# Loading residuals earlier and reordering the last block of an attention-plus-recurrence kernel

## The chip, the core and the metric

The kernel runs on one core of one Trainium2 chip. The metric is device time in microseconds (us) for one execution of the whole program. A core has five instruction queues that matter here: PE (TensorE, matrix products), DVE (VectorE), ACT (ScalarE), POOL (GpSimd), and SP, which only issues DMA transfers. Each queue runs its instructions strictly in order; an instruction that waits for another engine holds up all that stand behind it on its own queue.

## The reference

The input `x` has shape (4, 128, 64, 64): four batches, 128 channels, 4096 tokens each. Two layers are computed.

```
# layer 0: attention over tokens with 64-channel keys, queries, values; residual
q, k, v = wq @ x, wk @ x, wv @ x
x = x + wo @ (softmax(k.T @ q, over the second index) applied to v)

# layer 1, on tokens t of 128 channels
t = t + causal_attention(layernorm(t))          # 4096 tokens, 128 channels
w = layernorm(t) @ W.T                          # W is 128 x 128
w = (w - mean) * rsqrt(var + eps) * gamma + beta   # mean, var over all 4*4096 tokens
y[-1] = 0;  y[n] = sigmoid(w[n] + y[n-1] @ V.T)   # a recurrence over 4096 tokens
t = t + y
```

The last part couples everything: the normalization of `w` needs the statistics of all tokens of all batches, and the recurrence runs over all tokens.

## The kernel before, in words

**Attention.** For each batch the kernel first computes layer 0 and then layer 1. Scores are products on PE, exponentials run on ACT, row sums on DVE, and the second product runs on PE again. Layer 0 keeps three arrays per batch in the pool `batch`, made in `cols0`: `kr` (the keys and rows), `swap` (the same with its halves exchanged) and `v`. `finish1` ends a block of 512 tokens of layer 1: `first` normalizes and stores, `second` turns the block to channels by way of memory (`chans`, then `xhT`), `third` makes the product `wx_ps` with W and its statistics (`stats`). The sum x + attention, which the end needs again as residual, is stored to memory: by channel in `x2c` for batches 0 and 1 (`BY_C = 2`) and half of batch 2, by token in `x2t` for the rest. The memory pool frames decide where a buffer lies; waits are put in by a layer that follows which instruction writes and reads each region.

**The recurrence is cut up.** Each batch's 4096 tokens are divided into 256 chunks (`NCH`) of 16 steps (`STEPS`), and all chunks of a batch advance at once, so that one step of one batch is a 128x256 product. A chunk does not know its starting state. It is warmed up over some steps taken from the chunk before it; the map contracts fast, and the result is compared at the end against a tolerance (`judge`), with a slow general path for inputs where this fails. The steps come in three stages:

- *Early steps*, before the last block of the last batch is done. The statistics without that block are used (`ahead` makes `most` = scale, shift, shift_half and `near`, the scale as a diagonal matrix). There are `AHEAD = 3` of them, i = 0, 1, 2. A step i > 0 is `early_input` (product with `near`), `early_product` (product with V) and `early_sigmoid` (ACT). `WHOLE` lists the four parts whose data are there: batches 0, 1, 2 and seven eighths of batch 3. `LAST` is the remaining 32 columns of batch 3, which come out of `final_block`. Step 2 writes its states into `warmed`, which lies in the memory `joint`.
- *Warm steps* s = -6 to -1 in `step(b, s)`: product with V (`y_ps`, L1372), `z = scale * wx + product` on DVE (L1379), sigmoid with bias `shift` on ACT (L1383). They use the exact statistics of all tokens: `affine(mv, xrp, "all", False)` makes `scale` and `shift` after the last block. At s = -1 the state goes into `start`, and POOL copies a piece of it (L1385) before step 0 may begin.
- *Output steps* s = 0 to 15, the same three instructions for the four batches, and beside them `residual(s - 1)` (three transposes on PE at L1404, an addition on DVE at L1408, an output DMA) for the parts by token and `add(s)` (two additions on POOL at L1393 and L1395, output DMAs) for the parts by channel. From s = 1 on the order on every engine is the program's own (`pin` keeps an instruction in program order): steps of batches 0 to 3, then the residual.

**Order.** Instructions marked with `pin` keep their order. Others are placed by a scheduler in the layer that records the program, so the order on each engine is known from the built program and not from the source alone. `final_block` is written out by hand, all pinned:

```
early_product(2, *WHOLE[1])
product(0)
early_sigmoid(2, *WHOLE[1])
```

`product(k)` makes half k of the last block's product, its statistics (`ends`, L998) and a copy into `xs` on ACT (L1001).

**Loads of the end.** When the attention is over, SP issues the last block's stores, a first quarter of the by-token residuals `xr`, then `xc` (batches 0 and 1 by channel, two transfers of 2048 KB at L1331), then `xh` (1024 KB), then the rest of `xr`.

Of the kernel before, what the change touches and what calls it, by code (L numbers as in the profile page):

```python
# [369 lines left out]
def fast_path(  # L370
# [44 lines left out]
    xs = xpool.tile([P, B, N], F32, name="xs")  # L415


    x2c = dram.tile([P, BY_C * N + N // 2], F32, name="x2c")
    x2t = dram.tile([(B - BY_C) * N - N // 2, P], F32, name="x2t")
    by_c = lambda b, g: b < BY_C or b == BY_C and g < NB // 2  # L420
# [74 lines left out]
    grid = lambda t: t.rearrange("p (g c) -> p g c", c=CPB)  # L495
    pin = tc.keep_in_program_order

    def affine(mv, pool, name, halved=True):
# [3 lines left out]
        scale, shift, shift_half = one("scale"), one("shift"), halved and one("shift_half")  # L502
        nc.vector.tensor_scalar(var, mv[:, 1:2], BN_EPS, None, ALU.add)
        nc.gpsimd.tensor_tensor(y, var, mhalf[:, :1], ALU.pow)
        nc.vector.tensor_scalar(half, var, -0.5, None, ALU.mult)
        nc.vector.tensor_scalar(nmean, mv[:, 0:1], -1.0, None, ALU.mult)
        nc.vector.scalar_tensor_tensor(z, in0=y, scalar=half, in1=y, op0=ALU.mult, op1=ALU.mult)
        nc.vector.scalar_tensor_tensor(y, in0=z, scalar=1.5, in1=y, op0=ALU.add, op1=ALU.mult)
        nc.vector.tensor_tensor(scale, y, gamma, ALU.mult)
        if halved:  # L510
            nc.vector.scalar_tensor_tensor(
                shift_half, in0=nmean, scalar=scale, in1=beta_half, op0=ALU.mult, op1=ALU.add
            )
        nc.vector.scalar_tensor_tensor(shift, in0=nmean, scalar=scale, in1=beta, op0=ALU.mult, op1=ALU.add)
        return scale, shift, shift_half

# [10 lines left out]
    with tc.tile_pool(name="batch", bufs=1) as batch, tc.tile_pool(name="rows", bufs=2) as rowp, tc.tile_pool(  # L527
# [9 lines left out]
        def misc(name):  # L537
            return ps_m.tile([P, BLK], F32, tag="m", name=name)
# [37 lines left out]
        def cols0(b, m):  # L576

            bt = bs[b]  # L580
            if m == 0:
                bt.kr = batch.tile([P, 2, N // 2], F32, tag="kr", name="kr")
                bt.swap = batch.tile([P, N // 2], F32, tag="swap", name="swap")
                bt.v = batch.tile([P, NT // 2, 2, M], F32, tag="v", name="v0")
            for h, w in enumerate((wkq, wqk)):
                if (b, m, h) == (0, 1, 1):
                    ps = ps_a.tile([P, 2, BLK], F32, tag="a", name="kr_ps")[:, 0]
                else:
                    ps = misc("kr_ps")
# [207 lines left out]
        def early_place(i, b, g0, g1):  # L797

            if not early:
                early.extend(halves.tile([P, 2, BLK], F32, tag="half", name="early") for _ in range(AHEAD - 1))  # L800
                early.extend(ps_s.tile([P, 2 * BLK], F32, tag="s", name="early_ps") for _ in range(2))
            cols = slice(g0 * CPB, g1 * CPB)
            bank, half = (b - 1, 1) if g0 and i == AHEAD - 1 else (b, i % 2)
            at = early[AHEAD - 1 + bank % 2][:, ds(bank // 2 * BLK + half * NCH, NCH)][:, cols]
            return cols, at, by_step[:, b, i - AHEAD - WARM + STEPS, g0:g1]

# [5 lines left out]
        def early_product(i, b, g0, g1):  # L812

            cols, at, _ = early_place(i, b, g0, g1)
            pin(nc.tensor.matmul(at, lhsT=vf, rhs=early_states(i - 1, b)[:, cols], start=False, stop=True))  # L815
# [62 lines left out]
        def finish1(b, g, turn):  # L878
            agg, den = bs[b].agg, bs[b].den
            mem = {}  # L880

            def first():
                denominators(1, b, g, mem["own"])
                joined(1, b, g, mem["op"] if turn else projected1(agg))
                by_tokens(b, g)
                mem["xh"] = wk.tile([P, TPB, P], F32, tag="xh2", name="xh2")
                mem["of"] = moments(b, g)

            def norm():
                normed(b, g, mem["xh"], *mem["of"])  # L890

            def second():
                mem["xhT"] = wk.tile([P, BLK], F32, tag="xhT2", name="xhT2")
                chans = dram2.tile([P, BLK], F32, tag="chans", name="chans")
                stored(mem["xh"], chans)
                nc.sync.dma_start(out=mem["xhT"], in_=chans)

            def kept():

                stored(xs[:, b, ts(g, BLK)].rearrange("p (j c) -> p j c", c=P), x2c[:, ds(b * N + g * BLK, BLK)])  # L900

            def third():

                wp = misc("wx_ps")
                nc.tensor.matmul(wp, lhsT=wf, rhs=mem["xhT"], start=True, stop=True)  # L905
                nc.vector.bn_stats(stats[:, b * NB + g], wp)
                if b == B - 1 and g == NB - 2:
                    ahead()
                    in_range(False)
                nc.scalar.copy(xs[:, b, ts(g, BLK)].rearrange("p (s c) -> p s c", s=STEPS), wp.rearrange("p (c s) -> p s c", s=STEPS))  # L910

            def sums():
                mem["own"] = folded(den, g < 2)
# [27 lines left out]
        def final_block(b, g, agg, den):  # L941
# [72 lines left out]
            early_input(2, *WHOLE[1])  # L1014
            turned(1)
            early_product(2, *WHOLE[1])
            product(0)
            early_sigmoid(2, *WHOLE[1])
            early_input(2, *WHOLE[2])
            product(1)  # L1020
            in_range(True)
            early_product(2, *WHOLE[2])
            early_input(2, *WHOLE[3])
            early_product(2, *WHOLE[3])
            early_input(1, *LAST)
            early_input(2, *LAST)
            early_sigmoid(0, *LAST)
            for i in range(1, AHEAD):
                early_sigmoid(2, *WHOLE[1 + i])
                early_product(i, *LAST)  # L1030
                early_sigmoid(i, *LAST)

# [279 lines left out]
    with tc.tile_pool(name="xr", bufs=1) as xrp, tc.tile_pool(name="y", bufs=2) as yp, tc.tile_pool(  # L1312
# [8 lines left out]
        xc = xrp.tile([P, BY_C, NCH, STEPS], F32, name="xc")  # L1321
        xh = xrp.tile([P, P, STEPS], F32, name="xh")
        xr = xrp.tile([P, UNITS, STEPS, P], F32, name="xr")

# [2 lines left out]
                pin(nc.sync.dma_start(out=xr[:, m, part], in_=by_chunk(x2t)[:, m, part]))  # L1327

        load_by_token(slice(0, STEPS // 4))
        for b in range(BY_C):  # L1330
            pin(nc.sync.dma_start(out=xc[:, b].rearrange("p k s -> p (k s)"), in_=x2c[:, ts(b, N)]))  # L1331
        pin(nc.sync.dma_start(out=xh.rearrange("p k s -> p (k s)"), in_=x2c[:, ds(BY_C * N, N // 2)]))
        load_by_token(slice(STEPS // 4, STEPS))

        mv = xrp.tile([P, nc.vector.BN_AGGR_DIM], F32, name="mv")
        nc.vector.bn_aggr(mv, ends)
        scale, shift, _ = affine(mv, xrp, "all", False)
        start = xrp.tile([P, B, Q + 1, NCH // Q], F32, name="start")
        nc.gpsimd.memset(start[:, :, 0, 1:2], 0.0)
        ended = lambda b: start[:, b, 1:].rearrange("p q (g w) -> p g q w", g=NB)  # L1340
# [58 lines left out]
        def residual(s):  # L1399
# [8 lines left out]
            pin(nc.vector.tensor_tensor(t, t, ps, ALU.add))  # L1408
            pin(nc.sync.dma_start(out=by_chunk(out_t)[:, :, s], in_=t))

        met = ps_m2.tile([P, BY_C, NCH], F32, name="met")
        gap = xrp.tile([P, B], F32, name="gap")
        tol = xrp.tile([P, B], F32, name="tol")
# [4 lines left out]
        for s in range(-WARM, STEPS):  # L1418
            for b in range(B):
                step(b, s)  # L1420
            if s >= 1:
                residual(s - 1)
            if TPB <= s < TPB + BY_C:
                b = s - TPB
                pin(nc.scalar.copy(by_row(met[:, b]), ended(BY_C + b)))
            if 0 <= s < STEPS - 1:
                add(s)

# [30 lines left out]
        count = xrp.tile([P, B + 2], F32, name="count")  # L1459
        nc.vector.tensor_copy(count[:, B:], good)  # L1460

        def judge():
            total = xrp.tile([P, 1], F32, name="total")
# [87 lines left out]
```

## Time and profile before

| what | value |
|---|---|
| time, median of 4 runs | 2007.0 us (2006.48 to 2007.11) |
| profiled execution, its own time | 2006.34 us |
| its span, first to last instruction | 2004.6 us |
| granted TensorE clock | 1.000 |
| PE, DVE, ACT, POOL busy | 100%, 73%, 49%, 7% of the span |
| last attention instruction on ACT (exponential) | starts at 1939.32 us |
| first warm sigmoid on ACT (L1383) | starts at 1955.04 us |
| first output sigmoid (s = 0, batch 0) | starts at 1966.07 us |
| flag of `judge` written (L1470) | starts at 2001.18 us |

The profile page is a single execution, with times from its own first instruction. A busy engine in it is one on which an instruction is in flight; products overlap, so PE counts as busy even when it gives no more than a part of its rate. A row of the timeline has start, duration, engine, line, operation, tiles written and read, shapes and count, and in brackets the idle time before it with what ended that.

### The profile page before, as it was taken

The page shows a single profiled execution, that of the slowest core. Times are in us where ns is not written, and L with a number is a line of the kernel's source. Part 1 is how long each engine was busy: PE and PEld are TensorE (multiplying, and loading weights), DVE is VectorE, ACT ScalarE, POOL GpSimd, SP SyncE. Part 2 cuts the span into 40 slices and gives each one's busy share as a digit, 9 for nine tenths or more (in the row PEclk, how much of TensorE's full clock was granted, in tenths as well). Part 3 has the DMA queues.
Part 4 walks back from the last instruction along what each step waited for, and adds up shares of the span by engine and source line. Part 5 has one row for each costly group of instructions (what it writes and reads, how often), then busy time and mean ns, then how long its engine had stood idle before and what let it go on. Part 6 is the DMA issues. An engine that isn't in the chain of part 4 may idle for free.

```text
span 2004.6 us, 31348 instructions
## 1 busy us (share of the span) xinstructions
PE 1998.6 (100%) x11864; PEld 873.4 (44%) x11864; DVE 1456.4 (73%) x2823; ACT 973.7 (49%) x1053; POOL 142.8 (7%) x253
## 2 busy tenths in 40 slices
PE   9999999999999999999999999999999999999999
PEld 3333354444333345444433334444443333544457
DVE  5799877555789987655588998664468998774569
ACT  5666633332666653333466664323356666333348
POOL 0000011000000001000000001000000000110016
PEclk9999999999999999999999999999999999999999
DMA  3111112310110111320111111222010111120018
GB/s 106 44 33 23 22 33 59 78 28 16 43 52 15 23 23 38 71 73 16 43 22 59 23 18 27 55 64 58 16 44 2 23 23 23 33 54 17 17 51 308
DMA packets 220027, 89.03 MB, mean 44 GB/s; under 512 B 142688, under 2 KB 204512, under 8 KB 219488
## 3 DMA queue, kind: packets, MB, share of 16 engines
q1 hardware_dynamic: 219584, 86.82, 17.4%
q8 instruction: 94, 1.54, 0.3%
q14 instruction: 61, 0.50, 0.1%
q10 hardware_dynamic: 288, 0.16, 0.0%
HBM read 45.84 MB, written 36.89 MB: 41 GB/s over the span
## 4 chain that ended last, share of the span: by engine, by line
PE 99%; DVE 0%; ACT 0%; issue 0%; POOL 0%; ACTq 0%; POOLq 0%
PE s_ps L1080 23%; PE acc L1140 22%; PE s_ps L1065 22%; PE acc L1129 22%; PE y_ps L1372 2%; PE o_ps L694 1%; PE r_ps L653 1%; PE wx_ps L905 1%; PE kr_ps L590 1%; PE v_ps L602 1%; PE o_ps L704 1%; PE yT_ps L1404 0%; PE warm_ps L544 0%; PE early_ps L810 0%; PE early_ps L815 0%; PE vT_ps L628 0%
## 5 line engine op out<-in xcount | busy, mean ns | idle before, releaser
L1109 DVE TENSOR_TENSOR dsum<-dsum,p 128x1024 f32<-128x1024 f32 x692 | 845.0, 1221 | 399.1 <-ACT p L1083 293.0
L1074 ACT ACTIVATE p<-s_ps,nshift 128x1024 f32<-128x1024 f32 x512 | 569.7, 1116 | 310.8 <-PE s_ps L1065 284.0
L1083 ACT ACTIVATE p<-s_ps 128x1024 f32<-128x1024 f32 (+2 forms) x288 | 274.3, 952 | 605.3 <-PE s_ps L1080 581.3
L1129 PE MATMUL acc<-p,v 64*64 64x512 f32 x4096 | 527.9, 589 | 0.0
L1065 PE MATMUL s_ps<-kr,swap 64*64 64x512 f32 x2048 | 522.7, 590 | 0.0
L1065 PE MATMUL s_ps<-kr 64*64 64x512 f32 x2048 | 522.7, 590 | 0.0
L1080 PE MATMUL s_ps<-rows,xhT 128*128 128x512 f32 (+3 forms) x1152 | 500.4, 558 | 0.0
L1140 PE MATMUL acc<-p,xh 128*128 128x512 f32 (+3 forms) x1152 | 500.2, 557 | 0.0
L1080 PEld LDWEIGHTS s_ps<-rows,xhT 128*128 128x128 f32 x1152 | 215.2, 190 | 243.1 <-issue 202.4
L1140 PEld LDWEIGHTS acc<-p,xh 128*128 128x128 f32 x1152 | 216.1, 190 | 239.8 <-issue 223.4
L1129 PEld LDWEIGHTS acc<-p,v 64*64 64x64 f32 x4096 | 156.6, 133 | 282.8 <-issue 274.6
L1065 PEld LDWEIGHTS s_ps<-kr,swap 64*64 64x64 f32 x2048 | 141.6, 133 | 140.6 <-issue 132.5
L1065 PEld LDWEIGHTS s_ps<-kr 64*64 64x64 f32 x2048 | 141.6, 133 | 134.6 <-issue 132.3
L732 POOL TENSOR_TENSOR ln_rstd<-ln_var,mhalf 128x4 f32<-128x4 f32 x63 | 67.9, 1078 | 1178.7 <-DVE ln_var L730 1178.6
L1117 DVE TENSOR_TENSOR dsum<-dsum,p 128x256 f32<-128x256 f32 (+1 forms) x120 | 55.8, 498 | 61.6 <-POOL p L1089 61.6
L718 DVE SCALAR_TENSOR_TENSOR xs<-o_ps,recs,xs 128x128 f32<-128x128 f32 x252 | 69.3, 343 | 4.5 <-PE o_ps L704 1.7
L741 DVE TENSOR_SCALAR xh<-xs,ln_mv,ln_rstd 128x128 f32<-128x128 f32 x252 | 70.2, 342 | 2.0
L727 DVE BATCH_NORM_STATS2 ln_st<-xs 128x6 f32<-128x128 f32 x252 | 61.7, 271 | 0.0
L1089 POOL TENSOR_SCALAR_AFFINE_SELECT p<-p 128x128 f32<-128x128 f32 x128 | 34.4, 293 | 353.6 <-ACT p L1083 349.1
L1107 DVE COPY dsum<-p 128x1024 f32<-128x1024 f32 x44 | 30.2, 686 | 30.0 <-ACT p L1083 15.4
L755 DVE STREAM_TRANSPOSE sqT<-xh 128x512 f32<-128x512 f32 x63 | 44.7, 709 | 1.7
L664 DVE TENSOR_REDUCE part<-sq 128x16 f32<-128x512 f32 x64 | 41.7, 671 | 0.8
(171 smaller groups left out, 871.2 us busy)
## 6 DMA issues: line engine op xcount, KB each, us to landing
xs<-in_xT SPq DMA_DIRECT2D x32, 256.0 KB, 3.3
by_r<-sqT SPq DMA_DIRECT2D x128, 64.0 KB, 2.2
xhT<-by_r SPq DMA_DIRECT2D x128, 64.0 KB, 2.0
chans<-sqT SPq DMA_DIRECT2D x124, 64.0 KB, 1.8
xhT<-chans SPq DMA_DIRECT2D x31, 256.0 KB, 2.8
xs<-in_x SPq DMA_DIRECT2D x12, 512.0 KB, 5.4
x2c<-sqT SPq DMA_DIRECT2D x80, 64.0 KB, 1.8
swap<-kr SPq DMA_DIRECT2D x32, 128.0 KB, 2.3
```

What stands on the lines that cost most here:

```text
L718: nc.vector.scalar_tensor_tensor(t, in0=op[:, ts(j, P)], scalar=rec[:, j : j + 1], in1=t, op0=ALU.mult, op1=ALU.add)
L727: nc.vector.bn_stats(st[:, j], xs[:, b, ds(g * BLK + j * P, P)])
L732: nc.gpsimd.tensor_tensor(y, var, mhalf, ALU.pow)
L741: nc.vector.tensor_scalar(dst[:, j], xs[:, b, ds(g * BLK + j * P, P)], mv[:, j, 0:1], y[:, j : j + 1], ALU.subtract, ALU.mult)
L1065: ins = nc.tensor.matmul(ps[c * M : c * M + M, ts(r, BLK)], lhsT=keys[:, ts(c, M)], rhs=rows[r], start=True, stop=True,)
L1074: nc.scalar.activation(it.p, ps, AF.Exp, bias=nshift)
L1080: nc.tensor.matmul(ps[:, off : off + n], lhsT=lhsT, rhs=rhs, start=True, stop=True)
L1083: ins = nc.scalar.activation(it.p[:, :off], ps[:, :off], AF.Exp, scale=float(P) ** -0.5)
L1109: nc.vector.tensor_tensor(flat, flat, it.p, ALU.add)
L1117: nc.vector.tensor_tensor(den[:, h, q0:], den[:, h, q0:], it.p[:, o : o + n], ALU.add)
L1129: ins = nc.tensor.matmul(bt.acc[c * M : c * M + M, r], lhsT=bt.v[part, m * TPB + j, h], rhs=it.p[part, ts(c, BLK)], start=it.first, stop=i ...
L1140: ins = nc.tensor.matmul(bt.acc[:, 0, q0:], lhsT=bt.xh[:, t], rhs=it.p[:, o : o + n], start=it.first and h == 0, stop=it.last and h == 1,)
```

## The change

Three edits:

1. `kr`, `swap` and `v` of layer 0 become slices of one buffer `kept` of 2 x 4096 numbers for each partition, in a pool of its own. `xc` is allocated in the same memory, and its two loads are issued by `residuals(0)` and `residuals(1)`, at the start of `third` for blocks g = 5 and g = 6 of the last batch in layer 1. They leave the list of loads at the end.
2. In `final_block` the sigmoids of early step 2 come directly after their products; the inputs of `LAST` move down into the loop that uses them, and `LAST`'s piece of PSUM for i = 1 is another one. The sigmoid of step 2 for `WHOLE[1]` thereby passes `product(0)`, and that of `WHOLE[2]` stands before `LAST`'s products.
3. The exact affine is no longer made by `affine`. POOL makes `steep = y * gamma`, DVE makes `scale = (z + 1.5) * steep` in one instruction, and ACT makes `shift` by an activation `Identity`. The copy of `good` into `count` moves from DVE to ACT at s = 6.

```diff
+    keep = ctx.enter_context(tc.tile_pool(name="keep", bufs=1))
+    addends = []
...
-                bt.kr = batch.tile([P, 2, N // 2], F32, tag="kr", name="kr")
-                bt.swap = batch.tile([P, N // 2], F32, tag="swap", name="swap")
-                bt.v = batch.tile([P, NT // 2, 2, M], F32, tag="v", name="v0")
+                kept = keep.tile([P, 2 * N], F32, tag="kept", name="kept")
+                bt.kr = kept[:, :N].rearrange("p (r n) -> p r n", r=2)
+                bt.swap = kept[:, N : N + N // 2]
+                bt.v = kept[:, N + N // 2 :].rearrange("p (t h c) -> p t h c", h=2, c=M)
...
-            bank, half = (b - 1, 1) if g0 and i == AHEAD - 1 else (b, i % 2)
+            bank, half = (b - 1 if i == AHEAD - 1 else 0, 1) if g0 else (b, i % 2)
...
+            def residuals(k):
+                if not addends:
+                    addends.append(keep.tile([P, BY_C, NCH, STEPS], F32, tag="kept", name="xc"))
+                pin(nc.sync.dma_start(out=addends[0][:, k].rearrange("p k s -> p (k s)"), in_=x2c[:, ts(k, N)]))
+
             def third():
+                if b == B - 1 and g >= NB - 1 - BY_C:
+                    residuals(g - (NB - 1 - BY_C))
...
             early_product(2, *WHOLE[1])
+            early_sigmoid(2, *WHOLE[1])
             product(0)
-            early_sigmoid(2, *WHOLE[1])
             early_input(2, *WHOLE[2])
             product(1)
             in_range(True)
             early_product(2, *WHOLE[2])
+            early_sigmoid(2, *WHOLE[2])
             early_input(2, *WHOLE[3])
             early_product(2, *WHOLE[3])
-            early_input(1, *LAST)
-            early_input(2, *LAST)
             early_sigmoid(0, *LAST)
+            early_sigmoid(2, *WHOLE[3])
             for i in range(1, AHEAD):
-                early_sigmoid(2, *WHOLE[1 + i])
+                early_input(i, *LAST)
                 early_product(i, *LAST)
                 early_sigmoid(i, *LAST)
...
-        for b in range(BY_C):
-            pin(nc.sync.dma_start(out=xc[:, b].rearrange("p k s -> p (k s)"), in_=x2c[:, ts(b, N)]))
...
-        scale, shift, _ = affine(mv, xrp, "all", False)
+        nc.vector.tensor_scalar(var, mv[:, 1:2], BN_EPS, None, ALU.add)
+        nc.gpsimd.tensor_tensor(y, var, mhalf[:, :1], ALU.pow)
+        nc.gpsimd.tensor_tensor(steep, y, gamma, ALU.mult)
+        nc.vector.tensor_scalar(half, var, -0.5, None, ALU.mult)
+        nc.vector.tensor_scalar(nmean, mv[:, 0:1], -1.0, None, ALU.mult)
+        nc.vector.scalar_tensor_tensor(z, in0=y, scalar=half, in1=y, op0=ALU.mult, op1=ALU.mult)
+        nc.vector.scalar_tensor_tensor(scale, in0=z, scalar=1.5, in1=steep, op0=ALU.add, op1=ALU.mult)
+        nc.scalar.activation(shift, nmean, AF.Identity, scale=scale, bias=beta)
...
+            if s == TPB + BY_C:
+                pin(nc.scalar.copy(count[:, B:], good))
...
-        nc.vector.tensor_copy(count[:, B:], good)
```

**What the built programs show of the order.** All instructions before the last block stand in the same order on every engine, except for the two loads of `xc`, which now follow on SP the loads of `xhT` for blocks 5 and 6 of the last batch. At the end, PE's order becomes: the first warm product of batch 0; `LAST`'s step 1 (input, product); the warm products of batches 1 and 2; `LAST`'s step 2; the second warm products of batches 0 and 1; and only then the first warm product of batch 3. ACT's order becomes: both copies of `product`; step 2 of `WHOLE[2]`; step 0 of `LAST`; step 2 of `WHOLE[3]`; `shift`; step 1 of `LAST`; warm sigmoids of batches 0 and 1; step 2 of `LAST`; warm sigmoids of batch 2, batch 0 (second), batch 1 (second), batch 3 (first). Through the warm steps batch 3 thereby runs one place behind: each engine takes batch 3's step s between batch 1's and batch 2's step s + 1, until s = 1, from where the pinned order of batches 0 to 3 holds in both kernels.

More of the change, by code (lines that the diff above doesn't have):

```diff
@@ L496, in fast_path, with affine @@
     pin = tc.keep_in_program_order
-    def affine(mv, pool, name, halved=True):
+    def affine(mv, pool, name):
         one = lambda part: pool.tile([P, 1], F32, name=f"{name}_{part}")
         var, y, half, nmean, z = one("var"), one("y"), one("half"), one("nmean"), one("z")
-        scale, shift, shift_half = one("scale"), one("shift"), halved and one("shift_half")
+        scale, shift, shift_half = one("scale"), one("shift"), one("shift_half")
         nc.vector.tensor_scalar(var, mv[:, 1:2], BN_EPS, None, ALU.add)
@@ L509, in affine @@
         nc.vector.tensor_tensor(scale, y, gamma, ALU.mult)
[L510 to L513, printed above, removed]
+        nc.vector.scalar_tensor_tensor(
+            shift_half, in0=nmean, scalar=scale, in1=beta_half, op0=ALU.mult, op1=ALU.add
+        )
         nc.vector.scalar_tensor_tensor(shift, in0=nmean, scalar=scale, in1=beta, op0=ALU.mult, op1=ALU.add)
@@ L1320, in fast_path @@
         by_chunk = lambda t: t.rearrange("(m q s) c -> q m s c", q=P, s=STEPS)
-        xc = xrp.tile([P, BY_C, NCH, STEPS], F32, name="xc")
+        (xc,) = addends
         xh = xrp.tile([P, P, STEPS], F32, name="xh")
@@ L1336, in fast_path @@
         nc.vector.bn_aggr(mv, ends)
-        scale, shift, _ = affine(mv, xrp, "all", False)
+        one = lambda part: xrp.tile([P, 1], F32, name=f"all_{part}")
+        var, y, half, nmean, z = one("var"), one("y"), one("half"), one("nmean"), one("z")
+        steep, scale, shift = one("steep"), one("scale"), one("shift")
+        nc.vector.tensor_scalar(var, mv[:, 1:2], BN_EPS, None, ALU.add)
[6 more added lines that the diff above has]
+        nc.scalar.activation(shift, nmean, AF.Identity, scale=scale, bias=beta)
         start = xrp.tile([P, B, Q + 1, NCH // Q], F32, name="start")
@@ L1409, in residual @@
             pin(nc.sync.dma_start(out=by_chunk(out_t)[:, :, s], in_=t))
+        count = xrp.tile([P, B + 2], F32, name="count")
         met = ps_m2.tile([P, BY_C, NCH], F32, name="met")
@@ L1457, in fast_path @@
         tc.mark_branch_hint_location(BRANCH, "LikelyTaken", engines=mybir.ALL_ENGINES)
-        count = xrp.tile([P, B + 2], F32, name="count")
-        nc.vector.tensor_copy(count[:, B:], good)
         def judge():
```

## The prediction

> **What bounds the kernel now.** The page comes first. Its chain of waits puts everything on PE, which is true up to the last attention product near 1940 us and says little after it, since overlapped products count as busy.
>
> ```profile
> span 2004.6 us, 31348 instructions
> PE 99%; DVE 0%; ACT 0%; issue 0%; POOL 0%; ACTq 0%; POOLq 0%
> ```
>
> So I looked at stretches by the table of windows: one of layer 0 with a 2 MB load in it and the one after it, the warm steps, the output steps.
>
> ```profile
> 568.00:576.00 8.00, 8.00 (x80) 2.87 (x76) 5.96 (x5) 5.19 (x5) 0.00 (x0) 1.00 0.73 263
> 576.00:584.00 8.00, 8.00 (x104) 3.35 (x100) 6.53 (x13) 4.72 (x5) 0.00 (x0) 1.00 0.01 2
> ...
> 1956.00:1964.00 8.00, 8.00 (x37) 5.41 (x36) 7.91 (x18) 7.95 (x18) 0.00 (x0) 1.00 0.99 422
> 1970.00:1996.00 26.00, 26.00 (x141) 22.78 (x140) 26.00 (x65) 22.27 (x53) 25.04 (x27) 1.00 0.88 282
> ```
>
> The columns are PE, PEld, DVE, ACT and POOL busy (count), clock, DMA share and GB/s. From 1970 on DVE has no idle time: four `z` and one residual addition make a round of 2.055 us, and 14 rounds follow one another. Nothing that starts earlier on another engine shortens them; only the start of the first one moves the end. The waits agree: ACT waits for DVE once a round (4.2 us, 12 times).
>
> In the warm steps no engine is the limit. There ACT starts a batch's next sigmoid 1.813 us after its last (1955.044, 1956.857), which is the loop of one batch: sigmoid 0.508, product with its wait 0.79, `z` 0.48, and 0.035 to ACT. The four batches are four such loops side by side. What counts is the loop that is latest when the pinned order begins: batch 3. It starts last, because its last 32 columns come out of the last block through three sigmoids in a row. The timeline shows how that start comes about:
>
> ```profile
> 1952.11 0.37 ACT L1001 COPY xs<-wx_ps 128x256 f32<-128x256 f32 x1
> 1952.51 0.41 ACT L825 ACTIVATE early<-xs,most_shift_half,most_scale 128x32 f32<-128x32 f32 x1
> 1952.60 0.55 POOL L504 TENSOR_TENSOR all_y<-all_var,mhalf 128x1 f32<-128x1 f32 x1 [4.54 <-DVE all_nmean L506]
> 1953.18 0.22 DVE L507 SCALAR_TENSOR_TENSOR all_z<-all_y,all_half 128x1 f32<-128x1 f32 x1 [0.34 <-POOL all_y L504]
> 1953.43 0.16 DVE L508 SCALAR_TENSOR_TENSOR all_y<-all_z,all_y 128x1 f32<-128x1 f32 x1
> 1953.51 0.47 ACT L823 ACTIVATE joint<-early_ps,most_shift 128x256 f32<-128x256 f32 x1 [0.59 <-PE early_ps L810]
> 1953.62 0.16 DVE L509 TENSOR_TENSOR all_scale<-all_y,gamma 128x1 f32<-128x1 f32 x1
> 1953.82 0.22 DVE L514 SCALAR_TENSOR_TENSOR all_shift<-all_nmean,all_scale,beta 128x1 f32<-128x1 f32 x1
> 1953.88 0.28 ACT L823 ACTIVATE early<-early_ps,most_shift 128x32 f32<-128x32 f32 x1
> 1954.82 0.29 ACT L823 ACTIVATE joint<-early_ps,most_shift 128x32 f32<-128x32 f32 x1 [0.32 <-PE early_ps L815]
> 1955.04 2.32 ACT L1383 ACTIVATE y<-z,all_shift 128x256 f32<-128x256 f32 x5
> ```
>
> The 128x32 row at 1954.82 is batch 3's last early sigmoid. Its warm product follows on PE at 1955.162, its `z` at 1955.900, its sigmoid at 1956.416, 1.37 us after batch 0's. From there the chain is rigid: 12.855 us to batch 3's sigmoid of s = 1 at 1969.271, with the first residual addition on DVE at 1969.154.
>
> **Early loads.** Two 2 MB transfers leave the end and run after the `xhT` loads that SP issues at 1869.46 and 1918.02. In the windows above, 2 MB in 8 us leaves PE without idle time, as the quiet window does; 40 products of L1129 take 589 ns each there, the mean of the whole run. SP's next issues come at 1888.91 and 1946.49, so nothing queues behind them. The nearest work is `third`, whose product reads `xhT` at 1883.41 and 1930.89, 12.9 us or more after its issue; even behind a whole 2 MB it would land in 2.6 + 8.0 = 10.6 us. Cost 0. The gain is 0 as well, though a row seems to offer one:
>
> ```profile
> 1967.12 1.52 POOL L1393 TENSOR_TENSOR sum<-xs,xc 128x512 f32<-128x512 f32 x1 [0.85 <-DMA xh<-x2c]
> ```
>
> POOL's first addition seems to wait 0.85 us for a load, but it also needs batch 1's output sigmoid, which ends at 1967.043; without the load it starts as late. Later additions track ACT (the last one starts at 1997.90, its sigmoid ends at 1997.74), and nothing on the way to the flag waits for them. If the quieter DMA engines speed the loop, it shows as less than 1.813; no row separates that, so I allow 0.05 a step over seven steps, 0.3 us of gain, for the lower end. Sharing memory costs nothing: what `kept` newly waits for are transfers and copies of the batch before.
>
> **Early sigmoids.** ACT idles twice before 1955: 0.59 (for PE, which had `LAST`'s inputs ahead) and 0.32. Both go. `WHOLE[1]`'s sigmoid now runs near 1950.4, inside the 1.75 us in which ACT waits for the block's statistics, so the two copies keep their places at 1951.29 and 1952.11. `WHOLE[2]`'s sigmoid follows the second copy at 1952.37, the 128x32 one 0.37 later, `WHOLE[3]`'s at 1953.05. Then `shift` is next in line on ACT, and the rest of `LAST` stands behind it.
>
> **The affine.** Up to `all_z` (ends 1953.397) nothing changes. `steep` has no row. Below it lies POOL's smallest memset, 0.10, above it the power, 0.55; I take the copy at L1385, 0.21, nearest in kind to one multiplication: from 1953.20 to 1953.41. So `scale` starts at 1953.50, counting 0.07 for its second wait instruction (`z` starts 0.105 after its product in such a case, 0.039 otherwise), and ends at 1953.66 instead of 1953.78.
>
> The Trainium skill ("GPSIMD Engine Reference", Key points) speaks against this: elementwise work is about twice as slow on GpSimd as on VectorE. The copy row gives 0.213 against 0.159 for DVE's one-number multiplication, a factor of 1.3 at this size. By the rule an estimate of 0.32 for `steep` would delay `scale` by 0.05, and the sum below would be 0.55 instead of 0.5.
>
> `shift` on ACT starts at 1953.70. Between ACT's 0.28 (32 columns, one operand by pointer) and 0.41 (two by pointer, as here) I take 0.38; batch 0 hides it, as its sigmoid waits for `z` longer. No table is reloaded: the instruction order holds the same two table loads as before, the trace's at 1.79 and 1939.82 (1.28 us each).
>
> **The sum for batch 3.** Batch 0's product now stands ahead of `LAST`'s on PE and is done by 1953.3, so its `z` starts 0.10 after `scale`: 1953.76 to 1954.24, against 1954.32. Its sigmoid starts at 1954.34 (before: 1955.04), batch 1's 0.40 later at 1954.74. Both stand ahead of `LAST`'s last sigmoid, which therefore starts at 1955.14 and ends at 1955.43, instead of 1955.11. Then PE: batch 0's second product issues from 1954.90, batch 1's from 1955.33 (its sigmoid ends 1955.25), and batch 3's first one behind them at 0.432 for a product, at 1955.76. It ends 0.606 later, `z` takes 1956.41 to 1956.89, and the sigmoid starts at 1956.92 instead of 1956.416: 0.5 us late. Batches 0 to 2 are early by some 0.5 to 0.7 and gain nothing, since DVE, in the pinned order, takes batch 3's `z` of s = 1 before the residual and the next round.
>
> With 12.855 us of unchanged chain and saturated rounds, the end moves by +0.5: 2006.34 + 0.5 = 2006.8 for an execution like the profiled one. The median of the runs stands 0.66 above the profiled time, so 2007.5. With `steep` as slow as the power (ends 1953.75) all moves by 0.29 more: +0.8; without the extra waits of 0.07, twice, it is +0.36; with 0.3 from quieter DMA, +0.1. The copy into `count` hides in ACT's 0.35 of idle time a round, as the `met` copies (0.36) do.
>
> **Rivals.** *Forecast, 0.70:* batch 3 decides, 2007.5, own range 2006.9 to 2008.0. *Batch 0 decides, 0.20:* if the engines get through the round without waiting for batch 3, the end follows the earlier start (0.70 of ACT, less 0.2 for the small sigmoid now within the round): 2006.5. For it: batch 0's `z` begins 0.56 earlier. Against it: the order on DVE. *Load in the way, 0.05:* `xc` shares its memory rings with `xhT`; if `xhT` of block 6 lands after 1930.89, PE stops in the last block with its `third`, and the early stage's statistics and all after it move by the excess. It decides from a landing later than 12.9 us; two rates like the slowest `xc` landing (14.1 us, in the crowded end) after 2.6 give 16.7, 3.8 us late, 2010.8; a further delay passes 2011. Median landings of 2.6 speak against it. *The order is not what costs, 0.05:* memory placement or waits shift the attention by several us either way, for which no row speaks.
>
> A measurement of this kernel can tell about 0.2%, 4 us, from no change. The forecast and the batch 0 case lie within; slower by more takes the load (0.03 of its 0.05) or placement (0.02): 0.05; faster by more, placement alone (0.02); the same 0.93. The range runs from the batch 0 case to the forecast's upper end with a margin for the runs' spread: 2006.4 to 2008.2.
>
> **What would show it.** Right: the first warm sigmoid near 1954.3 and a fourth L1383 row only after the second ones of batches 0 and 1; batch 3's first one near 1956.9; an idle stretch of ACT of about 1 us near 1967 before the early sigmoid of batch 3; the first residual addition near 1969.66; rounds of 2.055; two 2 MB loads near 1870 and 1918 with PE at the same pace. Wrong: a first residual addition before 1969.15, or attention that ends later than 1939.3.

## The result, and the profile after

| | kernel before | changed kernel |
|---|---|---|
| median time | 2006.78 us (54 runs, 2006.05 to 2008.16) | 2010.45 us (34 runs, 2007.38 to 2011.52) |
| ratio of the means, 95% interval | 1 | 1.0015 [1.001, 1.002] |
| profiled execution: time, span | 2006.34, 2004.6 us | 2008.16, 2006.4 us |

By the medians the change costs 3.67 us where 0.5 were forecast. The profile of the changed kernel does not show such a loss, and that is the first thing to read from it: it is an execution of 2008.16 us, 2.3 below the median. The list of all executions says why. It gives time and span for 36, and the difference, the time *outside* the span, has two values: 1.73 to 1.93 us in 12 executions and 4.49 to 5.11 in 24. The two groups have medians of 2007.8 and 2010.7. Their spans do not differ (2005.5 to 2006.6 in both). The kernel before was 1.69 to 1.90 outside in all 93 executions listed beside the experiments below. So the loss has two parts: some 3 us outside the span in two executions of three, and something inside it.

Inside the span, the page says of the chain what it said before:

```profile
span 2006.4 us, 31342 instructions
PE 99%; DVE 0%; ACT 0%; issue 0%; POOL 0%; DVEq 0%; POOLq 0%; ACTq 0%
```

The table of windows (PE, PEld, DVE, ACT, POOL busy, clock, DMA share, GB/s) answers the one of before:

```profile
568.00:576.00 8.00, 8.00 (x80) 2.81 (x76) 5.79 (x6) 5.18 (x5) 0.00 (x0) 1.00 0.72 263
576.00:584.00 8.00, 8.00 (x104) 3.42 (x100) 6.46 (x11) 4.53 (x5) 0.00 (x0) 1.00 0.01 2
1956.00:1964.00 8.00, 8.00 (x36) 5.54 (x36) 7.27 (x18) 7.65 (x19) 0.00 (x0) 1.00 0.86 334
1970.00:1996.00 26.00, 26.00 (x140) 22.77 (x140) 25.89 (x64) 22.38 (x55) 25.03 (x26) 1.00 0.78 243
```

The DMA share at the end fell (0.99 to 0.86, 0.88 to 0.78), since 4 MB were moved away from there, and no time came of it. In the warm steps DVE and ACT are busy for less of the same 8 us: they wait more. The timeline shows for whom; `...` stands for rows left out.

```profile
1953.03 0.37 ACT L1011 COPY xs<-wx_ps 128x256 f32<-128x256 f32 x1 [0.45 <-DVE ends L1008]
1953.30 0.48 ACT L825 ACTIVATE joint<-early_ps,most_shift 128x256 f32<-128x256 f32 x1
1953.66 0.41 ACT L827 ACTIVATE early<-xs,most_shift_half,most_scale 128x32 f32<-128x32 f32 x1
1953.97 0.45 ACT L825 ACTIVATE joint<-early_ps,most_shift 128x224 f32<-128x224 f32 x1
...
1954.14 0.19 POOL L1350 TENSOR_TENSOR all_steep<-all_y,gamma 128x1 f32<-128x1 f32 x1
1954.45 0.16 DVE L1354 SCALAR_TENSOR_TENSOR all_scale<-all_z,all_steep 128x1 f32<-128x1 f32 x1
1954.64 0.39 ACT L1355 ACTIVATE all_shift<-all_nmean,beta,all_scale 128x1 f32<-128x1 f32 x1 [0.23 <-DVE all_scale L1354]
1954.86 1.26 DVE L1397 SCALAR_TENSOR_TENSOR z<-xs,all_scale,y_ps 128x256 f32<-128x256 f32 x3 [0.25 <-DMA xr<-x2t]
1954.94 0.27 ACT L825 ACTIVATE early<-early_ps,most_shift 128x32 f32<-128x32 f32 x1
...
1955.42 0.91 ACT L1401 ACTIVATE y<-z,all_shift 128x256 f32<-128x256 f32 x2 [0.22 <-ACT early L825]
...
1956.23 0.27 ACT L825 ACTIVATE joint<-early_ps,most_shift 128x32 f32<-128x32 f32 x1
1956.40 0.49 ACT L1401 ACTIVATE y<-z,all_shift 128x256 f32<-128x256 f32 x1
...
1956.72 3.16 DVE L1397 SCALAR_TENSOR_TENSOR z<-xs,all_scale,y_ps 128x256 f32<-128x256 f32 x7 [0.60 <-PE y_ps L1390]
...
1957.23 1.37 ACT L1401 ACTIVATE y<-z,all_shift 128x256 f32<-128x256 f32 x3 [0.34 <-DVE z L1397]
```

Times in this profile stand about 0.92 later than in the one of before, all along from the first product for `v` on (7.64 us against 6.72). To compare, every time is taken from the start of the second copy of `product` (1952.11 before, 1953.03 here; the differences are made from the trace's nanoseconds, the rows are rounded). Batch 0's first warm sigmoid is then at +2.40 (before +2.94). `LAST`'s last early sigmoid, the 128x32 row at 1956.23, is at +3.21 (before +2.72). Batch 3's first warm sigmoid, the third in the row at 1957.23, is at +5.07 (before +4.31). Its sigmoid of s = 0 ends an idle stretch of ACT (the first row is batch 2's sigmoid of s = 0, the second batch 3's):

```profile
1967.79 0.51 ACT L1401 ACTIVATE early<-z,all_shift 128x256 f32<-128x256 f32 x1
...
1969.25 0.51 ACT L1401 ACTIVATE early<-z,all_shift 128x256 f32<-128x256 f32 x1 [0.96 <-DVE z L1397]
...
1970.95 0.55 DVE L1426 TENSOR_TENSOR xr<-xr,yT_ps 128x384 f32<-128x384 f32 x1
```

In before the same two sigmoids follow one another without idle time:

```profile
1967.00 0.97 ACT L1383 ACTIVATE early<-z,all_shift 128x256 f32<-128x256 f32 x2
...
1969.15 0.55 DVE L1408 TENSOR_TENSOR xr<-xr,yT_ps 128x384 f32<-128x384 f32 x1
```

In the changed kernel ACT finishes batch 2 at 1968.29 and stands idle for 0.96 us until batch 3's `z` comes. The first residual addition is at +17.92 (before +17.05), and 14 rounds of 2.06 us follow as before. The tail is 0.87 us longer.

### The profile page after: what moved, and what is told of

It is laid out like the page before. It is cut to its first block, busy times and chain, and to the rows that moved or that the text cites. A ratio compares the mean times of both kernels' runs of the same rounds, so it can differ in the third digit from the quotient of the medians.

```text
span 2006.4 us, 31342 instructions
## 1 busy us (share of the span) xinstructions
PE 1999.7 (100%) x11864; PEld 874.2 (44%) x11864; DVE 1455.8 (73%) x2820; ACT 974.4 (49%) x1055; POOL 143.9 (7%) x254
## 4 chain that ended last, share of the span: by engine, by line
PE 99%; DVE 0%; ACT 0%; issue 0%; POOL 0%; DVEq 0%; POOLq 0%; ACTq 0%
PE s_ps L1090 23%; PE acc L1150 22%; PE s_ps L1075 22%; PE acc L1139 22%; PE y_ps L1390 2%; PE o_ps L696 1%; PE r_ps L655 1%; PE kr_ps L592 1%; PE wx_ps L915 1%; PE v_ps L604 1%; PE o_ps L706 1%; PE yT_ps L1422 0%; PE warm_ps L545 0%; PE early_ps L812 0%; PE early_ps L817 0%; PE vT_ps L630 0%
## 5 line engine op out<-in xcount | busy, mean ns | idle before, releaser
L1075 PE MATMUL s_ps<-kept 64*64 64x512 f32 x4096 | 529.3, 590 | 0.0
L1139 PE MATMUL acc<-p,kept 64*64 64x512 f32 x4096 | 527.9, 589 | 0.0
L1139 PEld LDWEIGHTS acc<-p,kept 64*64 64x64 f32 x4096 | 156.6, 133 | 282.9 <-issue 274.6
L1075 PEld LDWEIGHTS s_ps<-kept 64*64 64x64 f32 x4096 | 154.9, 133 | 275.2 <-issue 265.0
L920 ACT COPY xs<-wx_ps 128x512 f32<-128x512 f32 x31 | 18.1, 585 | 48.0 <-DVE stats L916 44.1
L1397 DVE SCALAR_TENSOR_TENSOR z<-xs,all_scale,y_ps 128x256 f32<-128x256 f32 x88 | 37.6, 477 | 2.3 <-PE y_ps L1395 1.0
```

Source lines behind the costliest of these rows:

```text
L1075: ins = nc.tensor.matmul(ps[c * M : c * M + M, ts(r, BLK)], lhsT=keys[:, ts(c, M)], rhs=rows[r], start=True, stop=True,)
L1139: ins = nc.tensor.matmul(bt.acc[c * M : c * M + M, r], lhsT=bt.v[part, m * TPB + j, h], rhs=it.p[part, ts(c, BLK)], start=it.first, stop=i ...
```

## The experiments

Two theories had to be tried: that the 0.87 us in the tail come from batch 3's late start and not from the loads or the affine as such, and that the 3 us outside the span come from where the compiled code of POOL ends and not from any work. For the second there was one clue: the compiled instruction streams of the two kernels differ by a few instructions for ACT, DVE and SP (fewer) and by one for POOL (448 instead of 447). The rival was that one of the edits does something that costs 3 us.

The measured values in one table. All positions are from the second copy on, in the profiled execution.

| kernel | median us | outside the span, us | `LAST`'s last early sigmoid | batch 3's first warm sigmoid | first residual addition | flag |
|---|---|---|---|---|---|---|
| before | 2006.71 to 2006.85 | 1.69 to 1.90 | 2.72 | 4.31 | 17.05 | 49.08 |
| changed | 2010.45 | 1.73 to 1.93 or 4.49 to 5.11 | 3.21 | 5.07 | 17.92 | 49.95 |
| e1, loads only | 2006.40 | 1.73 to 1.82 | 2.72 | 4.31 | 17.04 | 49.07 |
| e2, sigmoids only | 2007.09 | 1.69 to 1.89 | 3.01 | 4.84 | 17.67 | 49.71 |
| e3, affine only | 2009.88 | 4 of 10: 1.72 to 1.80; 6: 4.63 to 5.02 | 3.29 | 5.02 | 17.86 | 49.89 |
| e4, POOL 447 | 2007.26 | 1.69 to 1.87 | 3.20 | 5.07 | 17.92 | 49.95 |
| e5, `LAST` first | 2006.63 | 1.69 to 1.81 | 2.40 | 4.00 | 16.73 | 48.76 |
| e8, the same, old affine | 2006.49 | 1.71 to 1.87 | 2.41 | 4.00 | 16.79 | 48.82 |

**One edit at a time.** e1 takes only the early loads and the shared memory.

> Edit 1 alone (the early loads of xc into the memory of kept), on the kernel before. Two things are looked at apart: the span, and the time outside the span (execution time less span), which was 1.74 us in the profiled execution of the kernel before and 1.76 in that of the changed one, but about 4.7 in three quarters of the changed kernel's other executions. Theory (batch 3 in the last block, and code placement): span as the kernel before within 0.1 us in its tail (second copy of product to batch 3's sigmoid of s = 1: 17.17 us in before, 18.04 in the changed kernel), up to 0.3 less if quieter DMA helps; time outside 1.8, since POOL's instruction stream is as long as before's (447 instructions, the changed kernel has 448). Rival 1 (the loads or the shared memory cost): this run has the changed kernel's +3 us, wherever it lies. Rival 2 (it is the length of ACT's or SP's stream): ACT has 5 and SP 2 instructions fewer here than before, so 4.7 outside here.

Ratio 0.9998 [0.9988, 1.0007], no change in the tail, 1.8 outside: edit 1 costs and gains nothing. It also settles a row of the prediction. With the load long done, POOL's first addition still idles 0.85, now put down to ACT:

```profile
1967.19 1.53 POOL L1402 TENSOR_TENSOR sum<-xs,xc 128x512 f32<-128x512 f32 x1 [0.85 <-ACT xs L1392]
```

e2 takes only the order of the last block.

> Edit 2 alone (early sigmoids after their products, LAST's inputs moved down). Theory (batch 3 in the last block): LAST's last sigmoid now stands behind batch 0's first warm one, so batch 3 is late: second copy to batch 3's first warm sigmoid 4.5 to 4.8 us (before 4.31, changed 5.07), span +0.2 to +0.5; time outside 1.8, as POOL's stream has before's 447 instructions. Rival 1 (this edit alone makes the whole change in the tail): 5.07 and +0.8. Rival 2 (batch 0 decides): the span follows the earlier first warm sigmoid and falls by up to 0.2.

Ratio 1.0002 [0.9992, 1.0012]; the tail is 0.63 longer and batch 3 starts at +4.84, both above what was expected. Some 0.29 of it shows on ACT:

```profile
1954.56 0.51 ACT L1383 ACTIVATE y<-z,all_shift 128x256 f32<-128x256 f32 x1 [0.76 <-DVE z L1379]
1954.97 0.27 ACT L823 ACTIVATE joint<-early_ps,most_shift 128x32 f32<-128x32 f32 x1
```

ACT stands idle for 0.76 us for batch 0's `z`, and `LAST`'s last sigmoid waits behind it in the queue. Another 0.24 lie between that sigmoid and batch 3's first warm one (1.83 instead of 1.59).

e3 takes only the affine.

> Edit 3 alone (steep on POOL, scale in one DVE instruction, shift and the copy into count on ACT). Theory: in the tail, shift stands on ACT in place of an idle stretch, batch 3's early sigmoids keep their places: second copy to batch 3's first warm sigmoid 4.2 to 4.5 us (before 4.31), span -0.1 to +0.2. Outside the span: 4.7 us in most executions, if the length of POOL's stream (448 instructions, as the changed kernel; 447 before) is what costs 3 us there, so time +3. Rival (the 3 us belong to the early loads, to ACT's or SP's stream): 1.8 outside and no change of the time.

Ratio 1.0012 [1.0002, 1.0021]. Outside the span it did what the theory of the code says. In the tail the expectation failed: +0.81 instead of -0.1 to +0.2. The reason is the same kind of queueing:

```profile
1952.38 0.41 ACT L824 ACTIVATE early<-xs,most_shift_half,most_scale 128x32 f32<-128x32 f32 x1
1953.59 0.39 ACT L1346 ACTIVATE all_shift<-all_nmean,beta,all_scale 128x1 f32<-128x1 f32 x1 [0.80 <-DVE all_scale L1345]
1953.88 0.45 ACT L822 ACTIVATE joint<-early_ps,most_shift 128x256 f32<-128x256 f32 x1
1954.23 0.27 ACT L822 ACTIVATE early<-early_ps,most_shift 128x32 f32<-128x32 f32 x1
1954.40 0.44 ACT L822 ACTIVATE joint<-early_ps,most_shift 128x224 f32<-128x224 f32 x1
1954.75 0.51 ACT L1392 ACTIVATE y<-z,all_shift 128x256 f32<-128x256 f32 x1
1955.26 0.29 ACT L822 ACTIVATE joint<-early_ps,most_shift 128x32 f32<-128x32 f32 x1
```

In this order `shift` stands on ACT ahead of four early sigmoids and holds them for `scale`; the last of the four, `LAST`'s at +3.29, stands behind batch 0's first warm sigmoid too. The 0.63 of e2 and the 0.81 of e3 do not add up: together they give 0.87, as both act through the same sigmoid.

**The code that is never run.** e4 is the changed kernel with one line of the general path changed, which is compiled but not entered.

```diff
-                nc.gpsimd.tensor_tensor(o, xs[:, :, ts(kb, STEPS)], y.rearrange("p t b -> p b t"), ALU.add)
+                (nc.gpsimd if kb else nc.vector).tensor_tensor(o, xs[:, :, ts(kb, STEPS)], y.rearrange("p t b -> p b t"), ALU.add)
```

> The changed kernel whole, but in the general path, which is never entered with these inputs, one of 32 additions is given to DVE instead of POOL. Every instruction that is executed is the changed kernel's; POOL's stream gets one instruction shorter (447, as before), DVE's one longer. Theory (placement of the code behind the branch on POOL): time outside the span 1.8 in all executions, median 2007.5 (span +0.87, nothing else), 3 us less than the changed kernel. Rival (the work of the edits costs the 3 us): as the changed kernel, 4.7 outside in most executions, 2010.5.

All ten executions were 1.7 to 1.9 outside; ratio 1.0003 [0.9994, 1.0013]. The 3 us are gone, and the tail is the changed kernel's to 0.01. The next run does the reverse: it adds instructions to the general path of the kernel before.

```diff
+    idle = const.tile([P, 1], F32, name="idle")
+    for _ in range(1):
+        nc.gpsimd.memset(idle, 0.0)
```

> The kernel before with one more instruction, a memset of one number on POOL, in the general path that is never entered: POOL's stream has 448 instructions instead of 447, every other stream is before's, and every executed instruction is before's. Theory (placement on POOL): outside the span 4.7 us in about 3 of 4 executions, so a median near 2009.7, +3 against before, with the tail unchanged (first residual addition +17.05). Rival (something in the edits together with the length): 1.8 outside in all executions, no difference.

Median 2009.29, ratio 1.0008 [0.9999, 1.0018]: 1.73 to 1.81 outside in four executions, 4.59 to 5.07 in six, with the tail of before (+17.06, flag +49.09). The interval of the ratio still reaches 1; the time outside the span decides, as none of before's 93 executions has more than 1.90. So a kernel all of whose executed instructions are before's shows the loss. Three more runs change the 1 to 33, 2, 9 and 65, and one pads ACT and DVE instead (54 copies, 6 memsets).

> As the run before it, with 33 more instructions on POOL that are never executed: 480 instead of 447. It tells a threshold from one unlucky place. Threshold (any length from 448 on, up to some larger boundary, pays): 4.7 us outside the span in most executions, median near 2009.7. One place (the end lies exactly on a boundary of 64 instructions at 448): 1.8 outside, median 2006.7. I lean to the threshold, 6 in 10.

> The kernel before with two never-executed memsets on POOL: 449 instructions in POOL's stream. 448 cost 3 us outside the span in 6 of 10 executions, 447 and 480 nothing. If the end must lie exactly on a multiple of 64 instructions: 1.8 outside in all executions, median 2006.7. If the unlucky stretch is several instructions wide: 4.7 in most, median near 2009.3. I hold the first for likelier, 7 in 10.

> As the run before it with 456 instructions on POOL (nine more than before, never executed). If 449 is free, this one is free too: 1.8 outside, median 2006.7. If 449 pays, this tells whether the stretch reaches 8 instructions further (4.7 outside in most) or not (1.8).

> As the run before it with 512 instructions on POOL, the next multiple of 64 after 448 and a multiple of 128, which is what one instruction fetch of 8192 bytes brings at 64 bytes each. If any multiple of 64 is unlucky: 4.7 us outside in more than half of the executions, median above 2009. If only a length of 64 more than a multiple of 128 is (448 = 3 x 128 + 64): 1.8, median 2006.7. I give 5 in 10 to each.

> The kernel before with POOL's stream as before (447), but with never-executed memsets on DVE (8704 instructions instead of 8699) and copies on ACT (9472 instead of 9421), so that both streams end on a multiple of 64 instructions. If POOL alone has the unlucky place: 1.8 us outside, median 2006.7. If a stream of any engine that ends so costs: 4.7 outside in more than half of the executions. I give 6 in 10 to POOL alone.

| instructions in POOL's stream | kernel | executions about 3 us longer outside | median us | ratio |
|---|---|---|---|---|
| 447 | before | 0 of 93 | 2006.71 to 2006.85 | 1 |
| 448 | changed | 24 of 36 | 2010.45 | 1.0015 [1.0010, 1.0020] |
| 448 | e3 | 6 of 10 | 2009.88 | 1.0012 [1.0002, 1.0021] |
| 448 | e6 | 6 of 10 | 2009.29 | 1.0008 [0.9999, 1.0018] |
| 449 | e9 | 10 of 10 | 2009.76 | 1.0014 [1.0004, 1.0023] |
| 456 | e10 | 0 of 10 | 2006.75 | 0.9999 [0.9990, 1.0009] |
| 480 | e7 | 0 of 10 | 2006.56 | 0.9998 [0.9989, 1.0008] |
| 512 | e11 | 0 of 10 | 2006.86 | 0.9999 [0.9990, 1.0009] |
| 447, ACT 9472, DVE 8704 | e12 | 0 of 10 | 2006.60 | 0.9999 [0.9990, 1.0009] |

My guesses were half wrong: the unlucky place is neither a threshold (480 is free) nor exactly a multiple of 64 (449 pays always, 512 never). It is a short stretch that holds 448 and 449 and ends before 456. Two others of the five engines, brought to a multiple of 64, do nothing; other lengths of theirs were not tried.

The profiled executions of e9 and e10 fell one on each side. This is the view of DMA traffic for 2005.5 to 2011 us, after the last instruction of the span; the columns of a queue are packets, MB and share. First e9 (449, time 2010.15):

```profile
core 0 of [0], span 2004.7 us
...
DMA packets 6, 0.06 MB, mean 10 GB/s; under 512 B 0, under 2 KB 0, under 8 KB 0
...
q14 instruction: 5, 0.04, 2.8%
q8 instruction: 1, 0.02, 2.0%
```

Then e10 (456, time 2006.60):

```profile
core 0 of [0], span 2004.8 us
...
DMA packets 0, 0.00 MB, mean 0 GB/s; under 512 B 0, under 2 KB 0, under 8 KB 0
```

In the long execution the instruction queues fetch once more after the program's last instruction; in the short one they do not. The profiled executions of e3 and e6, 4.77 and 4.95 outside, show such fetches as well, and none of the eleven profiled executions with 1.7 to 1.8 outside does. Whether these fetches take the 3 us or only go with them was not shown. Why just these lengths cost, and whether it is POOL's length itself or the place that it gives to what is stored behind it, was not tried.

**The order again.** e5 keeps all three edits, has POOL at 447 by e4's line, and lets `LAST`'s chain go first; the diff is against the changed kernel. `last_early` collects the early sigmoids of steps 1 and 2; `issue_after` puts `shift` behind the last but one of them in ACT's order, and batch 0's first warm sigmoid behind the last. The first change of the diff gives `LAST` the piece of PSUM that it has in before.

```diff
-            bank, half = (b - 1 if i == AHEAD - 1 else 0, 1) if g0 else (b, i % 2)
+            bank, half = (b - 1, 1) if g0 and i == AHEAD - 1 else (b, i % 2)
...
+            early_sigmoid(0, *LAST)
             early_sigmoid(2, *WHOLE[2])
             early_input(2, *WHOLE[3])
             early_product(2, *WHOLE[3])
-            early_sigmoid(0, *LAST)
+            early_input(1, *LAST)
+            early_product(1, *LAST)
+            early_sigmoid(1, *LAST)
             early_sigmoid(2, *WHOLE[3])
-            for i in range(1, AHEAD):
-                early_input(i, *LAST)
-                early_product(i, *LAST)
-                early_sigmoid(i, *LAST)
+            early_input(2, *LAST)
+            early_product(2, *LAST)
+            early_sigmoid(2, *LAST)
...
+        with tc.issue_after(last_early[-2].ins):
+            nc.scalar.activation(shift, nmean, AF.Identity, scale=scale, bias=beta)
...
+            if (b, s) == (0, -WARM):
+                with tc.issue_after(last_early[-1].ins):
+                    nc.scalar.activation(y, shaped(z), AF.Sigmoid, bias=shift)
```

> All three edits, with POOL's stream at 447 instructions (as in e4), and the order of the last block changed: LAST's three early sigmoids come as early as their products allow (step 0 directly after the second copy, step 1 before step 2 of WHOLE[3], step 2 before batch 0's first warm sigmoid), shift after LAST's step 1. Theory (batch 3's chain sets the end, and the edits lost by putting batches 0 and 1 ahead of it): batch 3's first warm sigmoid 3.7 to 4.1 us after the second copy (before 4.31, e4 5.07), first residual addition at +16.5 to +16.8 (before +17.05, e4 +17.92), flag 0.3 to 0.5 earlier than before and 1.1 to 1.4 earlier than e4; median near 2006.3. Rival (the edits' extra waits, the slower affine on POOL or ACT, or the shared memory cost the 0.87, not the order): first residual addition stays at +17.7 to +17.9.

Every position came as expected: batch 3 at +4.00, first residual addition at +16.73, flag 0.32 earlier than before and 1.19 earlier than e4. The same edits, the same `steep` on POOL and `shift` on ACT, only another order. ACT no longer idles for `scale`, and `LAST`'s last sigmoid stands ahead of batch 0's:

```profile
1954.62 0.29 ACT L825 ACTIVATE early<-early_ps,most_shift 128x32 f32<-128x32 f32 x1 [0.35 <-PE early_ps L817]
1954.81 0.44 ACT L825 ACTIVATE joint<-early_ps,most_shift 128x224 f32<-128x224 f32 x1
1955.13 0.38 ACT L1358 ACTIVATE all_shift<-all_nmean,beta,all_scale 128x1 f32<-128x1 f32 x1
1955.50 0.29 ACT L825 ACTIVATE joint<-early_ps,most_shift 128x32 f32<-128x32 f32 x1
1955.68 0.50 ACT L1406 ACTIVATE y<-z,all_shift 128x256 f32<-128x256 f32 x1
```

The median is 2006.63 (expected 2006.3) against 2006.83 in the same session, ratio 0.9997 [0.9987, 1.0006]. The gain of 0.3 us is read from the positions; the whole time cannot tell it from nothing.

e8 is e5 without edit 3.

> As e5 in the order of the last block and with the early loads, but without edit 3: scale and shift are made on DVE as in the kernel before. Theory: batch 3 is no longer late, so the end is set by when scale and shift are ready; the first z starts at the place of before (2.2 us after the second copy, against 1.85 in e4), the fourth 3 x 0.475 later if LAST is in time: batch 3's first warm sigmoid at +4.0 to +4.3, first residual addition +16.8 to +17.05, flag 0 to 0.3 earlier than before and 0.2 to 0.5 later than e5. That would be what edit 3 is worth once the order is right. Rival (edit 3 is worth nothing in any order): same as e5.

Ratio 0.9999 [0.9989, 1.0008]. The expectation failed in its point: edit 3 is worth 0.06 us, not 0.2 to 0.5. In both kernels `LAST`'s last sigmoid stands at +2.40 (2.41), batch 3's first warm one at +4.00 and its last one, of s = -1, at +13.07: its chain is the same in either form of the affine. The 0.06 come in at s = 0 (+15.09 against +15.03), where batch 3 stands behind the other batches and batch 0's chain, whose first warm sigmoid is 0.07 later in e8 (+2.66 against +2.59), is 0.05 late. So with `LAST` first, batch 3 alone no longer sets the end.

## Why the prediction was wrong, and where it was right

**The failed step: the time outside the span.** The sum was made on the span, and "the median of the runs stands 0.66 above the profiled time, so 2007.5" carried over the 1.74 us outside it as a constant. That is where nearly 3 of the 3.67 us arose: the added `steep` makes POOL's stream 448 instructions long. Without that, e4 stands at 2007.26, 0.24 from the forecast and inside the range. That it is so near is partly luck: the base of 2007.0, the median of four runs, lies 0.29 above the 2006.71 of before in e4's session, and the term of 0.5 was too small. No row of the profile before spoke of it, as its time outside never varied. The fourth rival, that placement counts, had the right word but not the mechanism: it spoke of memory and of the attention, and the attention kept its pace: the 0.92 us by which the second copy is later are there at the first product for `v` already.

**The term of 0.5 for batch 3.** The mechanism was right: batch 3 decides, through `LAST`'s sigmoid behind the warm ones of batches 0 and 1 and through PE's two products ahead of batch 3's. The size was 0.87. By its own steps, from the second copy:

- `steep` took 0.19 (estimate 0.21), a factor of 1.2 over DVE's 0.16 and not the two that the Trainium skill ("GPSIMD Engine Reference", Key points) gives; `shift` took 0.39 (0.38); `scale` ended at +1.58 (forecast +1.56). All held.
- "Batch 0's `z` starts 0.10 after `scale`" was mis-sized: 0.25, which put batch 0's sigmoid 0.16 and `LAST`'s last one 0.17 later than forecast. The trace has four wait instructions of DVE's queue ahead of that `z`, one about every 0.1 us, from +1.46 to +1.78. None of them lasts over 0.05, so nothing still held them, and `z` follows the last by 0.06; the DMA that its row names is not what it waited for. In before the same four lie between +1.73 and +2.16, the first three starting while DVE makes `shift`, and only the last is held, by the product: the 0.10 after that product was carried over to `scale`.
- From `LAST`'s last sigmoid to batch 3's first warm one 1.78 were reckoned and 1.86 measured (1.59 in before, e5 and e8, where no product stands between).
- "12.855 us of unchanged chain" from there to batch 3's sigmoid of s = 1 measured 12.97. To the first residual addition the way is also longer, by 0.09 to 0.10, in e2 and e3, where batch 3 is late as well, and not in e1 and e5. The traces place it at one step: from its sigmoid of s = -2 to that of s = -1 batch 3 takes 1.96 in the changed kernel, 1.95 and 1.94 in e2 and e3, and 1.82 or 1.81 in before, e1 and e5; the next step gives back 0.03. In the three, batch 3's last warm step stands behind output step 0 of batch 0 (in the changed kernel of batch 1 too). In these rows of the changed kernel the first is batch 3's s = -2, the second step 0 of batches 0 and 1, the third batch 3's s = -1:

```profile
1965.36 0.51 ACT L1401 ACTIVATE y<-z,all_shift 128x256 f32<-128x256 f32 x1
...
1966.44 0.96 ACT L1401 ACTIVATE xs<-z,all_shift 128x256 f32<-128x256 f32 x2
...
1967.31 0.49 ACT L1401 ACTIVATE start<-z,all_shift 128x256 f32<-128x256 f32 x1
```

So 0.17 + 0.08 + 0.11 = 0.36 lead from 0.5 to 0.86, and 0.87 was measured.

**Right.** The loads cost nothing and gain nothing (e1). The two early idle stretches of ACT (0.59 and 0.32) went, for nothing. The forms announced came: the fourth warm sigmoid behind the second ones of batches 0 and 1, 0.96 us idle on ACT before batch 3's early sigmoid, rounds of 2.06. Batch 0's early start bought nothing, against the rival that it decides.

**The start.** The 0.92 us by which the profile after is later from its first product for `v` on is no part of the change. e6, e7 and e9 to e12 execute before's instructions and nothing else, and their second copies start between 1951.95 and 1953.14; the whole difference is there at the first product for `v` (6.56 and 7.76). Two single profiles cannot be subtracted over their whole length; a mark close to the change must be their zero.

## What to carry to other kernels

In a queue that runs in order, an instruction that is ready early is not free to go first: ask what it leaves behind it, and give the first place to the longest chain (here three small sigmoids), not to the largest pieces. Measure from a mark near the change, and set each execution's time beside its span: a loss outside the span is found by no view of the span. When a change adds an instruction and the time jumps by more than any term can explain, pad or shorten code that is never run before looking for a cause in the work.

## What the runs showed of the hardware that was not expected

- The time outside the span depends on the length of POOL's compiled stream: 1.7 to 1.9 us at 447, 456, 480 and 512 instructions; 4.5 to 5.1 in 36 of 56 executions at 448 (the changed kernel, e3 and e6); 4.5 to 5.5 in all ten at 449. In the long executions that were profiled, more instruction packets are fetched after the end (six in e9, of 8 KB on q14 and 16 KB on q8).
- The Trainium skill ("Runtime: NRT & Kernel Launch", Instruction fetch mechanics) says that crossing a fetch block is mostly hidden and that a block has 16 KiB. Here the fetch packets on q14 have 8 KB, and a length that differs by one or two instructions cost 3 us. That a block is crossed there was not shown.
- Executions of one kernel differ by over 2 us in their span (2004.3 to 2006.6 for before). Among the profiled executions of before, e6, e7 and e9 to e12, up to 1.2 us of that are there within the first 8 us of the program.
- Taking 4 MB of loads out of the last 50 us lowered the DMA share from 0.88 to 0.78 between 1970 and 1996 us and sped up no step: rounds took 2.06 us and the loop of a batch 1.81 in both.
